# A residual stream kept centered over channels in a two-layer hybrid block (state-space scan, attention, experts)

## The chip, the cores and the metric

The kernel runs on one core of one Trainium2 chip. The metric is the device time of one launch in microseconds. Five engines work side by side, each on its own instruction list, in order: TensorE (PE, matmuls; PEld are its weight loads), VectorE (DVE), ScalarE (ACT), GpSimd (POOL) and SyncE (SP). SP issues plain transfers; POOL issues those that add to what is already at their destination ("adds" below) and those that gather rows by index. All arithmetic is in float32.

## The reference

The input is x of shape (8, 256, 32, 32): 8 images, 256 channels, 1024 tokens each. Layer 0 is a selective-scan block and a feed-forward block, layer 1 is attention and a mixture of experts. Cut to what matters here:

```
x1 = x  + mamba(layernorm(x)) @ W_out        # layernorm "a"; scan over tokens, 512 x 16 states
x2 = x1 + gelu(layernorm(x1) @ W1 + b1) @ W2 + b2          # layernorm "f"
t  = x2 + attention(layernorm(x2)) @ Wo + bo               # layernorms "t" (here) and "x" (below)
n  = layernorm(t)
out = t + layernorm(n + sum of 2 experts of n) * gamma + beta   # layernorm "y"
```

Every layernorm runs over the 256 channels of one token: it subtracts the mean, squares, takes the mean of the squares, and multiplies by one over its root. The two experts are chosen once for each image, from the mean of n over its tokens.

## The kernel before

**Tiling.** Channels lie on the 128 partitions, two blocks of them (KC = 2). Tokens are cut in 16 chunks of 512 (CH; two for each image, chunk i = 2b + c), so an activation is a [128, 2, 512] tile of 512 KB. Such tiles come from one pool, `t4`, of 25 slots; a stream of work that needs slots declares how many it will hold at most (`Owner`). The scan keeps its products in 4 slots of another pool (`hb`).

**The recurrence sets the order.** The main loop (lines 2018 to 2051) walks over 16 chunks x 32 steps; a step is one of 16 states for half of the 512 inner channels. In each step DVE multiplies the inputs by B (`hb<-xm,bc`), scans over the tokens (`hb<-da_all,hb`), and multiplies by C (`hb<-hb,bc`); POOL adds the result to the accumulator `dx` in SBUF by a transfer; ACT makes the decays `da_all` two steps ahead; SP loads the rows B and C, spread over the partitions, two states ahead (`bc<-bc_d`).

**All else is fitted around it by a planner.** The rest of the program consists of Python generators ("streams"): `prologue` (layernorm a, input product, convolution, softplus, once a chunk), `park` (layernorm a and the gate for chunks 2 to 15, early, results to DRAM), `epilogue` (gate product, W_out, layernorm f, feed-forward, layernorm t), `attention` and `project_part` / `project_last` (Wo, layernorm x), `all_experts` and `finish` / `finish_last` (layernorm y, output). While the program is written out, a small model (lines 62 to 124) keeps a clock for each queue; each `yield` says when the stream may go on, and `advance` (line 1908) issues what is due between two DVE instructions of the recurrence. Where the model finds PE idle, `keep_warm` (line 1894) issues a small matmul without use ("warm"). The model's times fix only the order; on the chip, semaphores decide. `all_experts` (line 1979) starts the experts of an image once the `o` streams (project) of both chunks have ended.

**Four tables** (lines 266 to 269), one entry a chunk, say at which step the next chunk's prologue starts (FRONT), at which the gate is fetched (GATE), whether the convolution runs on PE instead of DVE (CONV, `conv_pe` against `conv_dve`: 12 multiply-adds on DVE), and whether a softplus term is added by transfers alone (SOFT: 3 adds for each half instead of 2, and no DVE instruction).

**The layernorm** (line 390) works with the channels on the partitions, so the mean is a matmul with a constant matrix (`mean_w`, 1/256), spread over all partitions at once; DVE subtracts it; ACT squares; eight small matmuls put the variance of 512 tokens into a 128 x 128 block; ACT and DVE make 1/sqrt there; four matmuls with `pick` spread it over the partitions again; DVE multiplies. For f, t and x outside the last chunk the input is a sum made by an add into SBUF, and is stored to DRAM for the next residual (`stored`); the square overwrites it, and so waits for that store (lines 409 to 411). The last chunk (i = 15) and the last image keep their sums in SBUF and add on DVE.

The input x enters the residual twice: layernorm a reads it, and `epilogue` adds it by a transfer (line 952: `pool.dma_start(out=x1, in_=x_v[b, :, :, tok], accum_op=ALU.add)`).

Of the kernel before, what the change touches and what calls it, by code (L numbers as in the profile page):

```python
# [17 lines left out]
P = 128  # L18
# [36 lines left out]
def hybrid_kernel(ctx: ExitStack, tc: tile.TileContext, a: dict, out: bass.AP):  # L55
# [131 lines left out]
    for q in range(4):  # L187
        pool.memset(pick[HD * q : HD * q + 1, q : q + 1], -0.5)
    eps_t = const.tile([P, 1], F32, name="eps_t")
# [28 lines left out]
    b1 = const.tile([P, HID // P], F32, name="b1")  # L218
# [8 lines left out]
    bo2 = const.tile([P, KC], F32, name="bo2")  # L227
# [8 lines left out]
    t_d, xf_d, x1_d = {}, {}, {}  # L236
# [29 lines left out]
    FRONT = (7, 1, 1, 1, 1, 10, 16, 3, 14, 1, 10, 1, 13, 1, 13)  # L266
    GATE = (20, 7, 29, 25, 29, 21, 20, 15, 18, 30, 25, 28, 25, 14, 26, 15)
    CONV = (0, 0, 1, 1, 1, 1, 0, 0, 0, 0, 0, 0, 0, 0, 0, 0)
    SOFT = (0, 1, 1, 1, 1, 1, 0, 0, 0, 1, 0, 1, 1, 0, 1, 0)
# [120 lines left out]
    def layernorm(  # L390
        tmp, bank, src, dst, name, gain=None, bias=None, sums=None, stored=None, centered=False
# [4 lines left out]
        if stored is not None:  # L396
            dst = yield from tmp.take(f"{dst}_{name}")
        if not centered:
# [6 lines left out]
            if stored is None:  # L405
                yield
        if stored is None:
            sq = yield from tmp.take(f"sq_{name}")
        else:
            yield max(stored, model.end)  # L410
            sq = src
        act.activation(sq, dst, AF.Square)
# [26 lines left out]
        yield  # L439
        if gain is None and sums is None:  # L440
            vec.tensor_tensor(dst, dst, ps.unsqueeze(1).to_broadcast([P, KC, CH]), ALU.mult)
        else:
            for k in range(KC):
                vec.scalar_tensor_tensor(
                    dst[:, k, :], dst[:, k, :], 1.0 if gain is None else gain[:, k : k + 1], ps,
                    ALU.mult, ALU.mult, accum_out=None if sums is None else sums[:, k, :],
                )
                if bias is not None:
                    vec.tensor_scalar(
                        dst[:, k, :], dst[:, k, :], bias[:, k : k + 1], None, ALU.add  # L450
                    )
        bank.put(ps)
        tmp.put(sq)
        return dst
# [21 lines left out]
    set_up, gates_ready = [], []  # L476
# [84 lines left out]
    def prologue(i: int):  # L561
# [7 lines left out]
        if i < PARK:  # L569
            yield sp.dma_start(xn, x_v[b, :, :, c * CH : (c + 1) * CH])  # L570
            yield from layernorm(mem, banks, xn, xn, f"a{i}")
# [257 lines left out]
    def park():  # L829

        for i in range(PARK, B * NCH):
# [6 lines left out]
            yield from layernorm(mem, banks, xn, xn, f"a{i}")  # L838
# [61 lines left out]
    def epilogue(i: int):  # L900
# [7 lines left out]
        while "sz" not in me:  # L908
# [21 lines left out]
        if last:  # L930
            yield sp.dma_start(x1, x_v[b, :, :, tok])
# [14 lines left out]
        yield  # L946
        mem.put(*y)
        if last:
            xn = yield from mem.take(f"x_{i}")
            yield from layernorm(mem, banks, x1, xn, f"f{i}")  # L950
# [1368 lines left out]
```

## Time and profile before

| what | value |
| --- | --- |
| time, median of 3 runs | 3439.8 us (3434.69 to 3441.22) |
| profiled execution: its own time / its span | 3450.06 us / 3448.1 us |
| DVE, PE, ACT, POOL busy | 3031.7, 3192.0, 2459.8, 1127.5 us |
| PE busy in warm matmuls (`warm<-mean_c,zero_c`) | 352.6 us |
| first recurrence step, last one | 77 us, 3062 us |
| attention of image 0 to 7, first matmul at | 666, 1012, 1364, 1727, 2092, 2467, 2835, 3151 us |
| routing of the last image (logits) | 3347 us |
| bytes moved by transfers | 642.22 MB |

The profile is one execution. A group row names line, engine, operation, output tile<-input tiles, shapes, the count, then busy time and the mean of one instruction, then how long the engine stood idle just before them and who ended that. Nearly all rows have line 98 or 95, that of the helper through which the planner issues, so the tile names tell what it is: `mu_f`, `mu_t`, `mu_x`, `mu_a` are the means of the layernorms, `var_…` their variances. DMA shares are the mean busy share of 16 engines; packets overlap a little, so that a short stretch can show more than 1.

### The profile page before, as it was taken

To read this page: it belongs to the slowest core of one execution; us is meant where nothing else is said; L and a number is where in the kernel's file an instruction comes from. 1 tells how busy PE (TensorE), PEld (TensorE's weight loads), DVE (VectorE), ACT (ScalarE), POOL (GpSimd) and SP (SyncE) were. 2 spreads that over 40 slices of the span, in tenths; PEclk is the share of its full clock that TensorE was granted. 3 is DMA by queue.
4 is the path that set the end of the run, shared out by engine and by line. 5 is a ranking of instruction groups with operands and counts; after the bars stand their busy time and mean duration, and the time that the engine had idled before them with its cause. 6 is when DMAs were issued, how large, how long until landed. Compare 5 with 4: busy or idle time off the path is not lost. (4 is left out here: it accounts for less than half of the span.)

```text
span 3448.1 us, 40234 instructions
## 1 busy us (share of the span) xinstructions
PE 3192.0 (93%) x14371; PEld 1355.8 (39%) x14371; DVE 3031.7 (88%) x3171; ACT 2459.8 (71%) x3550; POOL 1127.5 (33%) x1068
## 2 busy tenths in 40 slices
PE   7888889899999999999999998999999999999997
PEld 4544343433343334333443334334433343334343
DVE  5889999999999899999999999999999999972561
ACT  4665857578777887887778876887778768764643
POOL 0243224322542244233452244325542243311010
PEclk9889999899999999999999999999999999999999
DMA  3878999989998999898998989799889989971120
GB/s 105 222 170 204 213 224 214 226 206 228 196 206 185 210 203 218 181 210 198 228 207 188 221 196 222 187 215 207 193 189 209 202 191 199 225 160 61 32 77 23
DMA packets 233187, 642.22 MB, mean 186 GB/s; under 512 B 29520, under 2 KB 106000, under 8 KB 232976
## 3 DMA queue, kind: packets, MB, share of 16 engines
q0 software_dynamic: 138176, 371.52, 57.7%
q1 hardware_dynamic: 94800, 268.03, 23.5%
q8 instruction: 115, 1.88, 0.2%
q14 instruction: 96, 0.79, 0.1%
HBM read 253.33 MB, written 77.07 MB: 96 GB/s over the span
## 5 line engine op out<-in xcount | busy, mean ns | idle before, releaser
L95 POOL DMA_DIRECT2D dx<-hb x512 | 540.5, 1059 | 1567.2 <-DVE hb L98 1127.5
L98 ACT ACTIVATE da_all<-dt,vecs 128x512 f32<-128x512 f32 (+1 forms) x1024 | 698.1, 716 | 291.5 <-DVE hb L98 285.5
L98 DVE TENSOR_TENSOR hb<-xm,bc 128x1024 f32<-128x1024 f32 x512 | 617.0, 1205 | 28.1 <-DMA dx<-hb 27.5
L98 DVE TENSOR_TENSOR_SCAN hb<-da_all,state,hb 128x512 f32<-128x512 f32 x512 | 631.2, 1270 | 10.4 <-ACT da_all L98 10.4
L98 DVE TENSOR_TENSOR hb<-hb,bc 128x1024 f32<-128x1024 f32 (+1 forms) x512 | 624.9, 1220 | 0.0
L98 DVE TENSOR_TENSOR_SCAN hb<-da_all,hb 128x1024 f32<-128x1024 f32 x256 | 585.1, 2285 | 8.5 <-ACT da_all L98 8.5
L98 ACT ACTIVATE pt<-sc 128x1024 f32<-128x1024 f32 x512 | 494.2, 1017 | 84.3 <-PE sc L98 72.2
L98 POOL COPY state<-hb 128x2 f32<-128x2 f32 x256 | 339.3, 1332 | 238.1 <-DVE hb L98 211.0
L98 PE MATMUL warm<-mean_c,zero_c 128*128 128x256 f32 x1084 | 352.6, 446 | 63.6 <-ACT dt L98 13.8
L98 PE MATMUL sc<-qk,qk 32*128 32x512 f32 x2048 | 343.6, 644 | 21.9 <-ACT pt L98 18.2
L98 PEld LDWEIGHTS warm<-mean_c,zero_c 128*128 128x128 f32 x1084 | 205.7, 211 | 214.1 <-PE warm L98 80.5
L98 PE MATMUL num<-pt,v 128*32 128x512 f32 x2048 | 278.4, 614 | 11.9 <-DVE ot L98 11.8
L98 PE MATMUL fh<-x_f,w 128*128 128x512 f32 x480 | 232.4, 614 | 5.9 <-DVE x_f L98 3.2
L98 PE MATMUL den<-pt,ecb 128*32 128x512 f32 x1792 | 237.6, 601 | 0.0
L98 PE MATMUL facc<-fh,w 128*128 128x512 f32 x512 | 231.1, 598 | 5.4 <-ACT xp L98 1.7
L98 PE MATMUL re<-he,g 128*128 128x512 f32 x472 | 219.0, 609 | 6.5 <-ACT pt L98 2.3
L98 PE MATMUL he<-xe,g 128*128 128x512 f32 x448 | 217.6, 610 | 2.5 <-ACT he L98 2.2
L98 ACT ACT_TABLE_LOAD x159 | 204.0, 1283 | 3.5 <-PEq L2306 0.7
L98 PEld LDWEIGHTS sc<-qk,qk 32*128 32x128 f32 x2048 | 102.1, 183 | 211.9 <-ACT pt L98 93.0
L98 PEld LDWEIGHTS facc<-fh,w 128*128 128x128 f32 x512 | 95.0, 190 | 131.5 <-issue 118.8
L98 PEld LDWEIGHTS fh<-x_f,w 128*128 128x128 f32 x480 | 86.7, 192 | 138.3 <-issue 109.8
L98 PEld LDWEIGHTS re<-he,g 128*128 128x128 f32 x472 | 89.6, 195 | 126.5 <-issue 107.9
(376 smaller groups left out, 4326.7 us busy)
## 6 DMA issues: line engine op xcount, KB each, us to landing
bc<-bc_d SPq DMA_DIRECT2D x256, 512.0 KB, 4.9
dx<-hb POOLq DMA_DIRECT2D x256, 512.0 KB
dx<-hb POOLq DMA_DIRECT2D x256, 511.0 KB
dt<-e POOLq DMA_DIRECT2D x48, 512.0 KB
dt<-u POOLq DMA_DIRECT2D x30, 512.0 KB
sz_d<-sz SPq DMA_DIRECT2D x28, 512.0 KB, 4.4
sz<-sz_d SPq DMA_DIRECT2D x28, 512.0 KB, 11.4
xe<-xf_d SPq DMA_DIRECT2D x28, 512.0 KB
```

What stands on the lines that cost most here:

```text
L95: f(*args, **kw)
L98: return f(*args, **kw)
```

## The change

The residual is carried without its mean over the channels. Layernorm a subtracts the mean as before, but the centered x is also stored (`xc_d`) and is what `epilogue` adds. W_out, W2, Wo and the biases b2 and bo have their mean over the output channels taken out once, during setup, so all that is added to the residual is centered too; f, t and x then need neither the mean nor the subtraction, and their square goes to the destination tile instead of over the input, with no wait for the input's store. The mean of the true residual is a row of 512 numbers a chunk: layernorm a's mean, and the products of W_out's, W2's and Wo's column means (`wm_out`, `wm_2`, `wm_o`) with the same inputs, made by the new `means` on PE and ACT and put to DRAM (`mu_d`, three rows a chunk). `project` loads the first three, adds the last, and stores the total (`mus_d`). `finish` adds it, spread over the partitions, to the output as a further add; `project_last` adds it to t. The gain gamma of layernorm y goes from DVE's last step to ACT's scale beside beta in `finish`. `epilogue` may not begin before the weights are centered. The four tables have new entries. Some small constants share storage (`b1`, `bo2`).

```diff
-    FRONT = (7, 1, 1, 1, 1, 10, 16, 3, 14, 1, 10, 1, 13, 1, 13)
-    GATE = (20, 7, 29, 25, 29, 21, 20, 15, 18, 30, 25, 28, 25, 14, 26, 15)
-    CONV = (0, 0, 1, 1, 1, 1, 0, 0, 0, 0, 0, 0, 0, 0, 0, 0)
-    SOFT = (0, 1, 1, 1, 1, 1, 0, 0, 0, 1, 0, 1, 1, 0, 1, 0)
+    FRONT = (7, 1, 1, 4, 1, 12, 13, 1, 6, 1, 6, 1, 1, 1, 12)
+    GATE = (19, 7, 30, 22, 26, 19, 15, 19, 12, 30, 14, 30, 18, 22, 14, 13)
+    CONV = (0, 0, 1, 1, 1, 0, 0, 0, 0, 0, 0, 0, 0, 0, 0, 0)
+    SOFT = (0, 1, 1, 0, 1, 1, 0, 0, 0, 0, 0, 1, 0, 0, 1, 0)
...
-        if not centered:
+        if kept is not None:
+            mu = yield from bank.take(f"mu_{name}")
+            for k in range(KC):
+                for q in range(4):
+                    pe.matmul(
+                        mu[HD * q : HD * q + HD, :P], mean_w[:, :HD], src[:, k, q * P : q * P + P],
+                        start=(k == 0), stop=(k == KC - 1),
+                    )
+            yield
+            sq = yield from tmp.take(f"sq_{name}")
+            row = sq[:, 1, :P]
...
+            act.copy(row, mu[:, :P])
+            yield
+            for q in range(4):
+                pe.matmul(
+                    mu[:, q * P : q * P + P], pick[:, q : q + 1].to_broadcast([P, P]), row,
+                    start=True, stop=True,
+                )
+            landed = sp.dma_start(mu_row(kept, 0), row[::HD, :])
+            yield
+            vec.scalar_tensor_tensor(
+                dst, mu.unsqueeze(1).to_broadcast([P, KC, CH]), 2.0, src, ALU.mult, ALU.add
+            )
+            bank.put(mu)
+            yield model.end if kept < PARK else max(landed, model.end)
+            kept_at = sp.dma_start(xc_d[kept], dst)
+            src = dst
+        elif not centered:
...
-        if stored is None:
+            yield
+            src = dst
+        if kept is not None:
+            pass
+        elif src is dst:
             sq = yield from tmp.take(f"sq_{name}")
         else:
-            yield max(stored, model.end)
-            sq = src
-        act.activation(sq, dst, AF.Square)
+            sq = dst
+        act.activation(sq, src, AF.Square)
...
+    def means(bank, wm, tiles, name, row, bias=None, more=()):
+        ps = yield from bank.take(f"mean_{name}")
+        n = KC * len(tiles)
+        for d in range(n):
+            for q in range(4):
+                pe.matmul(
+                    ps[HD * q : HD * q + HD, :P], wm[:, d : d + 1].to_broadcast([P, HD]),
+                    tiles[d // 2][:, d % 2, q * P : q * P + P],
+                    start=(d == 0), stop=(d == n - 1 and not more),
+                )
+        for w, r in more:
...
+        yield
+        if bias is None:
+            act.copy(row, ps[:, :P])
...
+        bank.put(ps)
+        yield
...
-        while "sz" not in me:
+        while "sz" not in me or not centered_w:
             yield POLL
...
-            yield pool.dma_start(out=x1, in_=x_v[b, :, :, tok], accum_op=ALU.add)
+            yield
+            landed = pool.dma_start(out=x1, in_=xc_d[i], accum_op=ALU.add)
+            yield from means(banks, wm_out, y, f"m{i}", row)
+            mem.put(y[1])
+            mem.put(y[0], at=sp.dma_start(mu_row(i, 1), row[::HD, :]))
+            yield max(landed, model.end)
...
+        for w, wm, n in ((w_out, wm_out, ND), (w2, wm_2, HID // P), (wo, wm_o, KC)):
+            for k in range(n):
+                act.activation(
+                    w[:, k, :], w[:, k, :], AF.Identity, accum_out=wm[:, k : k + 1]
+                )
+            act.activation(wm, wm, AF.Identity, scale=1.0 / C)
+            act.activation(wm_neg[:, :n], wm, AF.Identity, scale=-1.0)
+            for k in range(n):
+                act.activation(
+                    w[:, k, :], w[:, k, :], AF.Identity, bias=wm_neg[:, k : k + 1]
+                )
+            yield
+        centered_w.append(True)
...
     def project(tmp, bank, b: int, c: int, x1, ot, n):
         xr = yield from tmp.take(f"xr_{n}")
+        yield sp.dma_start(xr[:12, 0, :P], mu_d[b * NCH + c].rearrange("n (q t) -> (n q) t", t=P))
+        row = xr[:, 1, :P]
+        yield from means(
+            bank, wm_o, [ot], f"o{n}", row, mean_b, [(pick3[:12, :], xr[:12, 0, :P])]
+        )
+        yield sp.dma_start(mus_d[b][c].rearrange("(q t) -> q t", t=P), row[::HD, :])
...
         sp.dma_start(xf_d[b][c], xf)
+        parts = yield from mem.take(f"parts_{n}")
+        yield sp.dma_start(
+            parts[:12, 0, :P], mu_d[b * NCH + c].rearrange("n (q t) -> (n q) t", t=P)
+        )
+        row = parts[:, 1, :P]
+        yield from means(
+            banks, wm_o, [ot], f"o{n}", row, mean_b, [(pick3[:12, :], parts[:12, 0, :P])]
+        )
...
+        landed = sp.dma_start(mu_s.rearrange("(q t) -> q t", t=P), row[::HD, :])
+        mem.put(parts, at=landed)
+        yield landed
+        pool.dma_start(
+            out=t, in_=mu_s.partition_broadcast(P).unsqueeze(1).to_broadcast([P, KC, CH]),
+            accum_op=ALU.add,
+        )
...
-        yield from layernorm(mem, banks, r, r, f"y{b}_{c}", V("gamma"), centered=True)
+        yield from layernorm(mem, banks, r, r, f"y{b}_{c}", centered=True)
         yield
         for m in range(KC):
-            act.activation(r[:, m, :], r[:, m, :], AF.Identity, bias=V("beta", m))
+            act.activation(
+                r[:, m, :], r[:, m, :], AF.Identity, bias=V("beta", m), scale=V("gamma", m)
+            )
         yield
         yield pool.dma_start(out=r, in_=t_d[b][c], accum_op=ALU.add)
+        mu_s = mus_d[b][c].partition_broadcast(P)
+        yield pool.dma_start(
+            out=r, in_=mu_s.unsqueeze(1).to_broadcast([P, KC, CH]), accum_op=ALU.add
+        )
```

The excerpt of `means` leaves out the two adds of further rows by `pick3`; W2's part of `epilogue` is changed in the same way as W_out's.

## The prediction

> **What bounds the kernel now.** I read the page's busy shares and slices first. VectorE (DVE) is at 88% of the span, and nearly full from the third slice to the 35th; the DMA engines are nearly full over the same slices; both drop in the last five.
>
> ```profile
> DVE  5889999999999899999999999999999999972561
> DMA  3878999989998999898998989799889989971120
> ```
>
> Busy time by stretch (us, PE, PEld, DVE, ACT, POOL, clock, DMA share, GB/s) turns this into three stages:
>
> ```profile
> 77.00:850.00 773.00, 679.95 (x3054) 328.76 (x3053) 725.58 (x721) 532.54 (x839) 243.25 (x246) 0.93 0.89 210
> 850.00:2000.00 1150.00, 1102.95 (x5146) 433.23 (x5144) 1105.87 (x1087) 902.39 (x1283) 447.49 (x404) 0.98 0.91 204
> 2000.00:3063.00 1063.00, 998.53 (x4350) 402.51 (x4350) 1008.18 (x1002) 809.07 (x1143) 403.06 (x369) 0.97 0.90 203
> 3063.00:3448.00 385.00, 356.21 (x1604) 157.07 (x1596) 155.58 (x299) 184.65 (x240) 32.00 (x34) 0.98 0.21 55
> ```
>
> From 77 to 3063 us DVE works 2839.6 of 2986 us (95%). PE looks as busy, but 352.6 us of the whole are its warm matmuls, which are filler. So the main stage runs at DVE's pace, with the DMA engines close behind; the last 385 us are a chain over PE with DVE mostly idle. The groups by shape price what the change touches on DVE (count | busy, mean ns | idle before):
>
> ```profile
> L98 DVE SCALAR_TENSOR_TENSOR xm<-xp,vecs,xm 128x512 f32<-128x512 f32 x144 | 97.7, 745 | 11.9 <-ACT xm L98 11.9
> L98 DVE SCALAR_TENSOR_TENSOR re<-re,vecs,var_y 128x512 f32<-128x512 f32 x28 | 19.5, 740 | 7.8 <-PE var_y L98 7.7
> L98 DVE TENSOR_TENSOR x_f<-x,mu_f 128x1024 f32<-128x1024 f32 x15 | 18.1, 1207 | 2.2 <-PE mu_f L98 2.2
> L98 DVE TENSOR_TENSOR tn_t<-fo,mu_t 128x1024 f32<-128x1024 f32 x15 | 18.1, 1206 | 1.6 <-PE mu_t L98 1.6
> L98 DVE SCALAR_TENSOR_TENSOR e<-u,e 128x1024 f32<-128x1024 f32 x14 | 17.1, 1222 | 6.8 <-ACT u L98 6.8
> L98 DVE TENSOR_TENSOR xf_x<-xr,mu_x 128x1024 f32<-128x1024 f32 x14 | 17.0, 1213 | 8.8 <-PE mu_x L98 7.7 <-issue 1.2
> ```
>
> The waits say that DVE is paced by itself: others wait for it, and it seldom for a transfer (the last line).
>
> ```profile
> ACT da_all L98 <- DVE hb L98: 285.5, 234, 9.1
> POOL dx L95 <- DMA dx<-hb: 236.7, 59, 8.2
> DVE hb L98 <- DMA dx<-hb: 27.5, 18, 3.4
> ```
>
> In the chain that ended last, the last token chunk's third layernorm and the routing after it stand in the open (start, us, what):
>
> ```profile
> 3336.85 2.00 PE mu_x L98 x4
> 3338.87 1.23 DVE xf L98
> 3340.12 1.06 ACT sq_x L98
> ...
> 3347.01 0.34 PE logits L98 x4
> ```
>
> **What the Trainium skill says.** "DMA: Bandwidth & Descriptors", section "Issuing engines are not separate DMA queues": transfers from SP and POOL run on the same 16 engines. The trace agrees: q0 (POOL) and q1 (SP) take 57.7% and 23.5% of one set of 16, so a new SP store competes with POOL's adds. "VectorE: DVE Perf Modes", section "The perf-mode tier table": fp32 tensor_tensor runs in the 1x mode, with a PSUM operand too. The trace agrees: 1024 columns cost 1207 ns with PSUM and 1205 ns without. "Perfetto Trace Analysis", section "Optimization Strategy": the most-contended engine can change from one regime of a kernel to the next. The trace agrees: DVE is at 95% until 3063 us and at 40% (155.58 of 385) after it.
>
> **The change, part by part.**
>
> *Subtractions.* f, t and x lose theirs: 44 in the main stage, 18.1+18.1+17.0 = −53.2 us of DVE. Layernorm a keeps one, as a scalar_tensor_tensor (1222 against 1215 ns): +0.1. The gain in y's last step moves into ACT's scale: 28 x 740 ns (19.5 busy) become 14 full-width multiplies at 1.21 = 17.0: −2.5.
>
> *Tables.* CONV[5] goes from 1 to 0: 12 taps on DVE x 745 ns = +8.9. SOFT goes to 0 for chunks 3, 9 and 12: 6 x 1222 ns = +7.3. DVE in all: −53.2+0.1−2.5+8.9+7.3 = −39.4. Do freed DVE microseconds shorten the stage? Chunks (one chunk is 32 recurrence steps) with 163 to 169 us of DVE lasted 168 to 179, those with 182 to 186 lasted 185 to 201: about one for one. I count them in full. DVE also waited 12.6 us ahead of these subtractions; a quarter of it I count as gone, −3, since the next instruction inherits most.
>
> *DMA.* A q0 packet of 4096 bytes took 334 ns and one of 2048 took 194, so a 512 KB add is 128 x 334/16 = 2.67 us of all engines, or 256 x 194/16 = 3.10 if cut at 2 KB. SP stores: 128 x 195/16 = 1.56. Added: 16 stores of centered x (25.0) and 14 broadcast adds of the mean row (2 KB source rows, 43.4). Saved: 6 adds by SOFT (−16.0), and 15 residual adds reading the 4 KB-contiguous copy instead of the input (−6.5). Net +46 us. The stretches give 773 x 0.89 + 1150 x 0.91 + 1063 x 0.90 = 2691 of 2986, a share of 0.90; it becomes 2737/2947 = 0.93. They hide behind DVE while the engines have room. Ten-microsecond slices of the packet records reach 1.08 (packets overlap), so full is about there: 0.83 of full goes to 0.86. DVE's waits for transfers (27.5 for dx<-hb, 5.4 and 4.0 ahead of the gate product and of xm x dt: 37 us) grow with the queue, 0.86/0.14 over 0.83/0.17, by a quarter: +9. Bounds: 0 if all hides, +46 if the DMA engines set the pace.
>
> *PE and ACT.* Mean rows: 16+32+12 = 60 small matmuls a chunk. The nearest row is the variance's eight 128x32x128 at 9.5/15 = 0.63 us, so 4.7; removed means 3 x 2.0. At the slower 1.09 seen for eight it is 8.2. So −1.3 to +2.2 a chunk, behind DVE. ACT gains four row copies of 0.31 us a chunk; a's Square now waits for a mean-row store, with da_all's exponentials queued behind it on ACT and DVE's scans behind those. Against that, the Squares of f, t and x no longer wait for a 512 KB store (x1m_d 6.9 us to landing). Unknown sign; +3, bounds −8 to +15.
>
> *POOL and SP.* Mean adds: 14 x 1.42 us of POOL (the x<-in_x row, also 2 KB pieces), less 6 x 1.06 and 15 x 0.36: +8 us on an engine at 33%. Behind each stand dx adds; they free hb. Six SP issues a chunk (0.4 each) go ahead of some bc loads, which are issued two states (four recurrence steps) early. Hidden; uncovered, they would cost 2.4 us a chunk.
>
> *Setup.* Centering 14 weight columns: 14 x (446+190+500) ns = 16 us of ACT near 307 us, W2's 9 us in one piece with da_all behind; two steps of decay (10 us) cover most: +3. At the start the packed mean (1.1 us against 3.8 at the cold clock) pays for ACT's row copy and the spread back: −0.5.
>
> *The end.* Last chunk: without mean and subtraction f saves 3092.84−3088.9 = 3.9, t 1.98+1.22 = 3.2, x 3340.12−3337.15 = 3.0. Mean matmuls queue ahead of the next matmuls: +0.7 (f), +1.9 (t: 32 x 0.079 against 1.22 of cover). Experts of the last batch start when project_last is done, and that now ends after a load, mean matmuls, a row store and both landings: about 10 us of the planner's time, which it fills with warm matmuls at some 60% that PE must really run ahead of the logits. I take +7 (floor 4: a 2.8 us small landing as for bc_d, plus 1). Sum −0.5, say 0; bounds −8 to +12.
>
> **Sum** on the profiled span 3448.1 (execution 3450.06): −39.4−3+9+3+3−0.5+0 = −28, giving 3420. That execution lies 10.3 us above the median 3439.8, so the median becomes 3412.
>
> **Rivals.**
> 1. *The DMA engines become the bound* (slower). Place: 350 to 3063 us. In 45% of ten-microsecond slices their share is already over 0.97. If they pace the steps, DVE's 39 us buy nothing and +46 comes onto the path, less some overlap: 3439.8+30 = 3470. It decides if they can't sustain 0.93. Against it: over 1600 to 1700 us the mean was 1.005 while DVE kept going.
> 2. *The planner gives it back.* The order is made anew and streams hold t4 buffers longer (xr and r through extra transfers); half the gain goes: 3439.8−6 = 3434, near no change.
> 3. *More is gained.* Without store waits f and t shorten each epilogue by some 8 us, attention starts earlier, and less of it hangs over into the last stage: attention of batch 6 ended at 3088, after the last step: 3390.
> 4. *That the change doesn't do what it says*: the subtraction of a is still there, so a quarter of the means stays; already in the sum.
>
> **Chances.** Forecast (3397 to 3429) 0.60; rival 1 0.14; rival 2 0.12; rival 3 0.14. Changes under 0.2% (6.9 us) can't be told from none. Faster 0.60+0.14+0.04 of rival 2 = 0.78; same 0.06; slower 0.14+0.02 = 0.16. Range: 0.60 + 0.12 + half of rival 3 makes eight in ten: 3390 to 3447; the forecast's own is 3397 to 3429.
>
> **What would show it.** Right: no mu_f, mu_t, mu_x groups; DVE near 2990 us in all; the last recurrence step 25 to 40 us before 3063; DMA share near 0.93; DVE's waits for dx<-hb under 50 us; a last stage of 385, with 10 us between xf and logits. Wrong: DVE idle in the main stage 30 us above its 146, behind DMA (rival 1) or behind ACT and PE (rival 2).

## Result and profile after

The changed kernel takes 3461.26 us (median of 4 runs, 3459.36 to 3467.59) where the kernel before took 3440.07 beside it: ratio 1.0062, 95% interval 1.0047 to 1.0078. It is 21 us slower; the forecast was 28 us faster, and the range ended at 3447. The profiled execution has a span of 3465.8 us, against 3448.1.

The page's slices of the changed kernel (DVE busy, DMA engines busy, in tenths) look like those of before: both nearly full up to the 35th slice.

```profile
DVE  5888999999899999999999989999899999952551
DMA  3887999989898999789997999799989998862140
```

The same stretches as in the prediction, cut at this kernel's own first and last recurrence step (us, PE, PEld, DVE, ACT, POOL, clock, DMA share, GB/s):

```profile
72.00:850.00 778.00, 679.56 (x3616) 333.68 (x3615) 718.36 (x717) 534.91 (x887) 259.69 (x243) 0.90 0.88 209
850.00:2000.00 1150.00, 1067.97 (x5448) 437.24 (x5447) 1087.34 (x1070) 896.00 (x1294) 445.68 (x402) 0.97 0.91 207
2000.00:3065.00 1065.00, 993.88 (x5121) 407.48 (x5124) 998.74 (x993) 813.72 (x1171) 420.82 (x374) 0.96 0.91 207
3065.00:3466.00 401.00, 374.30 (x1828) 170.49 (x1820) 149.63 (x292) 197.02 (x257) 41.75 (x43) 0.98 0.27 65
```

DVE works 2804.4 us in the first three rows, 35 less than the 2839.6 before. Yet they last 2993 us where they lasted 2986: DVE's idle time went from 146 to 189. The last stage went from 385 to 401. The groups by shape show that DVE's work changed as reckoned (count | busy, mean ns | idle before):

```profile
L98 DVE TENSOR_TENSOR hb<-xm,bc 128x1024 f32<-128x1024 f32 x512 | 616.2, 1203 | 62.7 <-DMA dx<-hb 35.1 <-issue 27.4
L98 DVE SCALAR_TENSOR_TENSOR xm<-xp,vecs,xm 128x512 f32<-128x512 f32 x156 | 105.8, 743 | 10.3 <-ACT xm L98 10.3
L98 DVE SCALAR_TENSOR_TENSOR e<-u,e 128x1024 f32<-128x1024 f32 x20 | 24.9, 1243 | 5.4 <-ACT u L98 5.4
L98 DVE TENSOR_TENSOR re<-re,var_y 128x1024 f32<-128x1024 f32 x14 | 17.0, 1213 | 8.9 <-PE var_y L98 8.5
```

The groups of mu_f, mu_t and mu_x are gone. The first row is where idle time appears: DVE stood 62.7 us ahead of the product that opens a recurrence step, 28.1 us in the kernel before:

```profile
L98 DVE TENSOR_TENSOR hb<-xm,bc 128x1024 f32<-128x1024 f32 x512 | 617.0, 1205 | 28.1 <-DMA dx<-hb 27.5
```

The waits (engine, what it waited for: us, times, longest) say the same from the other side: POOL waits 334 us for its own additions into dx, 237 before.

```profile
POOL dx L95 <- DMA dx<-hb: 334.2, 86, 10.0
ACT da_all L98 <- DVE hb L98: 338.3, 229, 8.8
DVE hb L98 <- DMA dx<-hb: 35.1, 17, 5.7
DVE hb L98 <- issue: 27.4, 11, 5.2
```

In the chain that ended last (start, us, what), the routing of the last image has lost the mean product and the subtraction, and gained a wait for the row of means:

```profile
3351.19 1.06 ACT xf L98
...
3356.02 1.32 DVE xf L98 x4
3357.38 3.31 PE warm L98 x14
3360.69 0.92 PE mean_o L98 x24
3361.62 2.93 PE warm L98 x12
3364.55 0.36 PE logits L98 x4
```

From the start of the Square to the logits it is 13.4 us; before, from the start of the mean product to the logits, 10.2.

### The profile page after: what moved, and what is told of

Its sections match the earlier page's. It is cut to its first block, busy times and chain, and to the rows that moved or that the text cites. A ratio compares the mean times of both kernels' runs of the same rounds, so it can differ in the third digit from the quotient of the medians.

```text
span 3465.8 us, 44262 instructions
## 1 busy us (share of the span) xinstructions
PE 3166.2 (91%) x16259; PEld 1381.6 (40%) x16259; DVE 2990.6 (86%) x3134; ACT 2472.3 (71%) x3656; POOL 1169.6 (34%) x1078
## 4 chain that ended last, share of the span: by engine, by line
PE 34%; DVE 26%; DMA 14%; ACT 14%; issue 9%; POOL 2%; DVEq 0%; SPq 0%; POOLq 0%; ACTq 0%
DVE hb L98 20%; DMA dx<-hb 13%; PE warm L98 4%; PE sc L98 3%; PE num L98 3%; PE fh L98 3%; PE he L98 3%; ACT L98 3%; PE re L98 3%; ACT da_all L98 2%; PE facc L98 2%; DVE xm L98 2%; PE den L98 2%; ACT fh L98 2%; PE halves L98 1%
## 5 line engine op out<-in xcount | busy, mean ns | idle before, releaser
L98 DVE TENSOR_TENSOR hb<-xm,bc 128x1024 f32<-128x1024 f32 x512 | 616.2, 1203 | 62.7 <-DMA dx<-hb 35.1
L98 POOL COPY state<-hb 128x2 f32<-128x2 f32 x256 | 375.4, 1470 | 218.5 <-DVE hb L98 201.5
L98 PE MATMUL warm<-mean_c,zero_c 128*128 128x256 f32 x1020 | 339.7, 453 | 56.2 <-ACT dt L98 15.6
L98 PEld LDWEIGHTS warm<-mean_c,zero_c 128*128 128x128 f32 x1020 | 193.9, 213 | 201.2 <-PE warm L98 78.6
L98 PE MATMUL he<-xe,g 128*128 128x512 f32 x448 | 223.5, 624 | 10.2 <-ACT he L98 5.0
```

What stands on the lines that cost most here:

```text
L98: return f(*args, **kw)
```

## Experiments

Ratios are to the kernel before on the same chip, with 95% intervals; microseconds worked out from them use 3440 us. The stages named below are read from DVE's recurrence steps in each trace: chunk 0, chunks 1 to 15, and what follows the last step.

In most of the kernels the order of the instructions is held. `planned(f, ...)` lets the planner cost an instruction as ever but doesn't issue it (`plain` issues it as usual); an instruction issued through `nc.vector` or `nc.gpsimd` is one that the planner doesn't know of. So every other instruction stays where it was in its queue, and one part of the change is measured without a new plan.

The expectations name the theories by letters: T, the added transfers lost the time; O, the order and the tables; S, chunk 0 and the last stage; A, the pace of ACT and PE; P, the new products on PE; W, the change's own work on PE and ACT.

### The added transfers, in the changed kernel's order

```diff
-        yield pool.dma_start(
+        yield planned(
+            pool.dma_start,
             out=r, in_=mu_s.unsqueeze(1).to_broadcast([P, KC, CH]), accum_op=ALU.add
         )
```

> The changed kernel with the 14 additions of the mean row in finish costed in the plan but not issued, so every other instruction keeps its place in its queue; the outputs of images 0 to 6 lack their means. Theory T (the added transfers queue up and give the gain back): these adds are the dearest of the new transfers, 14 x about 2.9 us of all 16 DMA engines, bunched where the experts of an image finish; the time falls by 12 to 35 us, to about 3426 to 3449, and the waits for transfers in chunks 1 to 15, 77 us in the changed kernel, fall to 40 to 60. Theory O (the new order and tables lost the time): within 6 us of 3461. Theory S (the first chunk and the last stage lost it): within 8 us of 3461, since the last stage holds few of these adds.

Measured: 1.0016 (1.0004 to 1.0029), 16 us under the changed kernel's 1.0062, inside theory T's 12 to 35.

```diff
-            kept_at = sp.dma_start(xc_d[kept], dst)
+            kept_at = planned(sp.dma_start, xc_d[kept], dst)
...
-            landed = pool.dma_start(out=x1, in_=xc_d[i], accum_op=ALU.add)
+            landed = pool.dma_start(out=x1, in_=x_v[b, :, :, tok], accum_op=ALU.add)
```

> The changed kernel with the 16 stores of the centered x costed in the plan but not issued; the residual is added from x itself, so the layernorms f, t and x see an x that is not centered and the output is wrong by that. Theory T: 16 x about 2 us of all DMA engines, but most of it before 980 us, while the parked chunks are made; the time falls by 3 to 15 us, to 3446 to 3458. Theories O and S: within 5 us of 3461.

Measured: 1.0042 (1.0026 to 1.0058).

The third kernel does both, and each small load and store of a row of means is `planned` too, with the small products that read a loaded row.

> The changed kernel with none of the transfers that the change added: no additions of the mean row, no stores of the centered x (the residual is added from x), no mean rows stored or loaded. Their plan stays, PE's and ACT's work for the means too; the means are missing from the outputs. Theory T: back to the gain that the freed DVE time should give, less chunk 0 and the last stage: 3415 to 3440, waits for transfers in chunks 1 to 15 near the 36 us of the kernel before. Theories O and S: no lower than 3450.

Measured: 1.0012 (1.0003 to 1.0021). So the transfers cost 0.50%, 17 us, in this order, and nearly all of it is the 14 additions of the mean row (16 us); leaving out the stores alone gives 7 us back, with an interval that reaches nothing. Theory T had 21 to 46 us for all of them, theories O and S at most 11; neither holds. Without any of them the kernel is still no faster than before, with 41 us less work on DVE. The transfers are most of the 21 us by which the changed kernel is slower, but only a third of the 49 us by which it missed the forecast. Most of DVE's idle time ahead of the opening product stays without them, 49.4 of 62.7 us:

```profile
L106 DVE TENSOR_TENSOR hb<-xm,bc 128x1024 f32<-128x1024 f32 x512 | 615.9, 1203 | 49.4 <-DMA dx<-hb 25.2
```

### The subtractions and their mean products, in the order of before

```diff
+            skip = name[0] in "ftx"
             for k in range(KC):
-                pe.matmul(mu, mean_w, src[:, k, :], start=(k == 0), stop=(k == KC - 1))
+                (planned if skip else plain)(
+                    pe.matmul, mu, mean_w, src[:, k, :], start=(k == 0), stop=(k == KC - 1)
+                )
             yield
-            vec.tensor_tensor(dst, src, mu.unsqueeze(1).to_broadcast([P, KC, CH]), ALU.subtract)
+            (planned if skip else plain)(
+                vec.tensor_tensor, dst, src, mu.unsqueeze(1).to_broadcast([P, KC, CH]),
+                ALU.subtract,
+            )
```

> The kernel before with the mean products and the subtractions of the layernorms f, t and x costed in the plan but not issued (48 of each; the layernorms leave the mean out). No transfer is added and nothing moves: this is the freed DVE time alone. If DVE is the bound of the recurrence, as the prediction had it, 53 us less on DVE give 40 to 56 us: 3385 to 3400. If transfers, PE and ACT bound the stage as much, less than half of it: 3415 or more.

The mean products go with the subtractions (94 us in PE's groups), and the squares go to the destination tile, with no wait for the input's store. Measured: 0.9916 (0.9902 to 0.993), 29 us: just over half of the 54 us by which DVE's busy time fell (3031.7 to 2977.6). From 3440 us that is 3411, in neither theory's range and nearer to the second's. The stage from chunk 1 to the last step (columns as above), in the kernel before:

```profile
322.00:3062.00 2740.00, 2573.40 (x11398) 1041.77 (x11398) 2616.12 (x2529) 2085.19 (x2970) 1002.59 (x926) 0.97 0.92 206
```

and without the subtractions:

```profile
322.00:3040.00 2718.00, 2518.57 (x11214) 1016.09 (x11218) 2567.85 (x2486) 2078.15 (x2970) 967.43 (x926) 0.96 0.92 208
```

DVE has 48 us less to do, and the stage is 22 us shorter: its idle time went from 124 to 150 us. Is it the transfers that take the other half? Two kernels leave out the 42 additions in finish, one with and one without the subtractions:

```diff
-        yield pool.dma_start(out=r, in_=y, accum_op=ALU.add)
-        yield pool.dma_start(out=r, in_=xf_d[b][c], accum_op=ALU.add)
+        yield planned(pool.dma_start, out=r, in_=y, accum_op=ALU.add)
+        yield planned(pool.dma_start, out=r, in_=xf_d[b][c], accum_op=ALU.add)
...
-        yield pool.dma_start(out=r, in_=t_d[b][c], accum_op=ALU.add)
+        yield planned(pool.dma_start, out=r, in_=t_d[b][c], accum_op=ALU.add)
```

> The kernel before with the three additions in finish (of the other expert's part, of xf and of t_d; 42 in all, some 2.9 us of all DMA engines each, 122 us) costed in the plan but not issued; the outputs of images 0 to 6 lack these terms. A control for the next kernel: what these transfers cost while DVE does all its subtractions. Theory T (transfers wait only where they crowd): 5 to 20 us less than 3445. Theory A (the stage is paced by ACT and PE once DVE has less to do): 0 to 10 us less.

> The kernel before without the mean products and subtractions of f, t and x (as in the run before_no_subtraction, which gave 0.9916 of the time before), and without the 42 additions in finish. If transfers ate the other half of the 53 us of DVE time (theory T), the subtractions are worth more here than the 29 us they were worth with all the additions: 38 to 50 us against the kernel before with fewer adds. If ACT, PE or the order took it (theory A), they are worth 22 to 33 us here too.

Measured: 0.9945 (0.9925 to 0.9965) and 0.9845 (0.9827 to 0.9864). The additions alone are worth 19 us, in theory T's range. Without them the subtractions are worth 1.0%, 34 us with 9 either way, just above theory A's range; the interval reaches theory T's too, and the 29 us of before. Even with 127 us less for the DMA engines to do (packet times 2808.8 to 2681.4 us), some 20 us of the freed 54 are not gained.

### Chunk 0 and the last stage

Chunk 0 lasted 258 us in the changed kernel's trace and 245 before; the last stage was 15 us longer. Two kernels took one suspect each. In the first the mean of layernorm a goes to DVE by the old way:

```diff
-                    pe.matmul(
+                    planned(
+                        pe.matmul,
                         mu[HD * q : HD * q + HD, :P], mean_w[:, :HD], src[:, k, q * P : q * P + P],
                         start=(k == 0), stop=(k == KC - 1),
                     )
+                nc.tensor.matmul(mu, mean_w, src[:, k, :], start=(k == 0), stop=(k == KC - 1))
...
-            vec.scalar_tensor_tensor(
+            planned(
+                vec.scalar_tensor_tensor,
                 dst, mu.unsqueeze(1).to_broadcast([P, KC, CH]), 2.0, src, ALU.mult, ALU.add
             )
+            nc.vector.tensor_tensor(
+                dst, src, mu.unsqueeze(1).to_broadcast([P, KC, CH]), ALU.subtract
+            )
```

> The changed kernel with the mean of the layernorm a made as in the kernel before: two products with the column of 1/C straight into the bank that DVE subtracts from, in place of eight products, a copy on ACT and four products; the plan is held, the copy of the row stays but off the path of DVE, and the rows stored are wrong. Theory S (chunk 0 lost 13 us because DVE now waits for a product, a copy and a second product ahead of each parked x): chunk 0 back to 244 to 250 us from 258, the time 6 to 14 us less than the changed kernel's, ratio 0.2 to 0.4 per cent lower. Theories T and O: within 4 us of the changed kernel.

Measured: 1.0043 (1.0027 to 1.0059), chunk 0 251 us. The gap to 1.0062, 7 us, is at the lower end of theory S's 6 to 14, but within the two intervals, and chunk 0 took 250 to 254 us in the first three kernels too, which have the longer route. So the route is not shown to cost anything. The 258 us stand beside a granted TensorE clock of 0.83 in that stretch; the only other trace with so long a chunk 0 (259 us, the next kernel) has 0.83 too, and the 18 others have 0.86 to 0.92 and 242 to 254 us. A part of the 13 us may be the clock of that one execution.

In the second the row of means of image 6 is made after its layernorm x:

```diff
-        yield sp.dma_start(xr[:12, 0, :P], mu_d[b * NCH + c].rearrange("n (q t) -> (n q) t", t=P))
-        row = xr[:, 1, :P]
...
-        yield sp.dma_start(mus_d[b][c].rearrange("(q t) -> q t", t=P), row[::HD, :])
+        if not late:
+            yield from mean_row(xr)
...
         tmp.put(xf, at=sp.dma_start(xf_d[b][c], xf))
+        if late:
+            parts = yield from tmp.take(f"parts_{n}")
+            yield from mean_row(parts)
+            tmp.put(ot, parts)
```

> The changed kernel with one thing moved, and for image 6 alone: the row of means of the projection (load of the parts, products, copy, store) after the layernorm x and not ahead of the products with Wo. Everything up to the projection of chunk 14 keeps its order. Theory S (this row and its two transfers hold back the logits of image 6 by 29 us, and its experts then run inside the last attention): the logits of image 6 come at about 50 us after the last step in place of 77, the last attention ends about 10 us earlier, the last stage is 381 to 388 us in place of 395, the time 6 to 13 us less than the changed kernel's. Otherwise: within 4 us.

Measured: 1.005 (1.0034 to 1.0066); the last stage didn't get shorter (400 us by its trace, 395 in the changed kernel's). The products with Wo came 17 us earlier, but the logits of image 6 came 75 us after the end of the last step, hardly sooner than the changed kernel's 77 (the kernel before has 48): the new plan put other streams in between. Theory S fell in this part.

### The plan

What had not been taken apart was the order itself. Four kernels are planned afresh. The first has the changed kernel's code and the four tables of before:

```diff
-    FRONT = (7, 1, 1, 4, 1, 12, 13, 1, 6, 1, 6, 1, 1, 1, 12)
+    FRONT = (7, 1, 1, 1, 1, 10, 16, 3, 14, 1, 10, 1, 13, 1, 13)
...
```

> The changed kernel with the four tables FRONT, GATE, CONV and SOFT of the kernel before; all else as in the change. Theory O (the new tables lost the time): ratio 0.994 to 1.001. Theories T, S and P (the added transfers, chunk 0 and the products for the rows lost it): the tables of before were not made for this program, ratio 1.003 to 1.015.

Measured: 1.02 (1.0178 to 1.0222), beyond the ranges of all theories. With the tables of before the changed program is 47 us slower than with its own, so it isn't the new tables taken alone that lost the time. The second is the kernel before with the subtractions really taken out of the code, so that the plan knows of it:

```diff
-        if not centered:
+        skip = name[0] in "ftx"
+        if not centered and not skip:
             mu = yield from bank.take(f"mu_{name}")
```

> The kernel before without the mean products and subtractions of f, t and x, as in the run before_no_subtraction (0.9916), but with the plan made for it, so that the other queues are ordered for the shorter DVE work; the means are missing from its layernorms. If it was the held order that gave only 29 of the 53 us (theory O): 0.984 to 0.989. If ACT, PE and the transfers pace the stage as much as DVE does (theory A): 0.989 to 0.995.

Measured: 1.0062 (1.0043 to 1.0081). The same work in the held order took 0.9916. The new plan alone made 1.5%, 50 us; neither theory had that. The stage from chunk 1 to the last step grew from 2718 to 2792 us, and DVE's idle time in it from 150 to 213:

```profile
317.00:3109.00 2792.00, 2567.49 (x11572) 1050.88 (x11572) 2578.38 (x2498) 2094.67 (x2990) 984.00 (x929) 0.96 0.90 204
```

The third and fourth are a version that carries the means on PE and needs no large transfer: the mean of x is taken off in the bank of W_out's product, and the rows of means come back in the bank of an uncentered Wo's product.

```diff
+    def add_row(ps, picks, rows):
+        for q in range(4):
+            pe.matmul(
+                ps[:, q * P : q * P + P], picks[:, q : q + 1].to_broadcast([picks.shape[0], P]),
+                rows, start=False, stop=(q == 3),
+            )
...
                     ps, w_out[:, d, m * P : (m + 1) * P], y[d // 2][:, d % 2, :],
-                    start=(d == 0), stop=(d == ND - 1),
+                    start=(d == 0), stop=False,
                 )
+            add_row(ps, pick1[:4, :], rows)
```

> A version with the means carried by PE and not by transfers, with the tables of the kernel before. The residual stays x (no store of a centered x): each product with the centered W_out adds a bank row of minus the mean of x (four products over a 4-row tile, from the stored row), so that f and t need no mean and no subtraction; the product with an uncentered Wo adds the three stored rows of means (four products over a 12-row tile), so that t_d holds the whole sum, finish adds nothing more, and x keeps its mean and subtraction. 32 of the 48 subtractions are gone and the transfers added are rows of 2 KB. If a freed subtraction is worth the 0.6 us that the run before_no_subtraction gave (29 us for 48), 32 give 19 us, less 4 to 10 us for the mean rows on PE and ACT: ratio 0.993 to 0.998. If the mean products and the longer stages on PE (theory P) cost as much as they free: 0.999 to 1.004.

> The same version with the four tables of the changed kernel. By theory O (the tables move the time by 10 us or more) it differs from the run with the tables of before by more than 0.3 per cent; else by less.

Measured: 1.0327 (1.0305 to 1.0349) and 1.0371 (1.0345 to 1.0397). Both are slower than either kernel, the first far beyond both its ranges, with DVE idle 242 and 230 us in chunks 1 to 15; they differ by 0.4%, as theory O had it. Since these runs change work and plan at once, they don't tell what carrying means on PE is worth.

Then the bare question: how much does the time hang on the order, when the work is the same? One entry of FRONT, by one step:

```diff
-    FRONT = (7, 1, 1, 1, 1, 10, 16, 3, 14, 1, 10, 1, 13, 1, 13)
+    FRONT = (7, 1, 1, 1, 1, 11, 16, 3, 14, 1, 10, 1, 13, 1, 13)
```

> The kernel before with one entry of FRONT moved by one step: the prologue of chunk 6 starts at step 11 of chunk 5 and not at step 10. The work is the same. By theory O the plans that follow differ and with them the time, by 0.3 per cent or more, more likely slower since the tables of before were set for its own plan; by theory W within 0.2 per cent.

> The changed kernel with its entry of FRONT for chunk 5 moved by one step, 12 to 13. By theory O it differs from the changed kernel's 1.0062 by 0.3 per cent or more, either way; by theory W within 0.2 per cent.

(In the second, 12 became 13 in the changed kernel's table.) Measured: 1.0247 (1.0233 to 1.0262) and 1.0193 (1.0176 to 1.021). Both are as theory O had it. One step on one entry costs the kernel before 85 us, four times what the change did; DVE has the same 3171 instructions, PE 164 more warm matmuls (1248 for 1084). The stage of the first:

```profile
317.00:3124.00 2807.00, 2605.27 (x11532) 1067.94 (x11536) 2620.02 (x2535) 2085.36 (x2975) 1016.61 (x927) 0.97 0.89 202
```

DVE's 2620 us are those of before (2616); its idle time is 187 us and not 124. The new idle time has no single source. Of DVE's waits (0.6, 4.0 and 2.7 us in the kernel before):

```profile
DVE hb L98 <- issue: 15.5, 5, 5.6
DVE xm L98 <- DMA dt<-u: 15.3, 2, 9.7
DVE x L98 <- PE mo L98: 12.3, 2, 12.1
```

A few stream steps stand where what they need comes late, and DVE stands with them. The lengths of the chunks are those of before up to chunk 4; from chunk 5, whose entry it was, nine of eleven are longer, the worst (chunk 13) 216 us in place of 182.

### The order apart from the work

One kernel has the order of the changed kernel and nearly the work of before; the next has the same without the subtractions.

```diff
-            act.copy(row, ps[:, :P])
+            planned(act.copy, row, ps[:, :P])
...
             sq = dst
+            nc.vector.tensor_tensor(
+                dst, src, zero_c.unsqueeze(2).to_broadcast([P, KC, CH]), ALU.subtract
+            )
-        act.activation(sq, src, AF.Square)
+        act.activation(sq, dst if sq is dst else src, AF.Square)
```

> The changed program's order and tables with nearly the work of the kernel before: of what the change added, the additions of the mean row, the stores of the centered x, all rows of means (products, copies, stores and loads) and the centering of the weights are costed in the plan but not issued, and the mean route of a is that of before; of what it took away, the 48 subtractions of f, t and x are issued again, uncosted, each a DVE instruction of the same size ahead of the square (their mean products are not). What is left of the change is the order. Theory O (the order lost it): 3465 to 3490, ratio 1.004 to 1.011. Theory W (the change's own work on PE and ACT lost it, the order is neutral): ratio 0.997 to 1.003.

> The same without the 48 DVE instructions. The subtractions should be worth 20 to 35 us here too. Against no_added_transfers (1.0012) it leaves out the rows' products and copies, the centering and the longer route of a: by theory O that is worth under 8 us, ratio 0.998 to 1.002; by theory W 20 us or more, ratio 0.990 to 0.995.

Measured: 1.0182 (1.0167 to 1.0197) and 1.0022 (1.0012 to 1.0032). The first, all three stages:

```profile
73.00:324.00 251.00, 207.14 (x1120) 116.60 (x1119) 222.76 (x280) 150.36 (x285) 87.47 (x89) 0.89 0.75 183
324.00:3094.00 2770.00, 2516.99 (x11008) 1013.84 (x11012) 2629.94 (x2544) 2071.60 (x2960) 1052.08 (x920) 0.95 0.89 203
3094.00:3505.00 411.00, 376.76 (x1660) 169.53 (x1652) 155.73 (x297) 195.87 (x252) 34.41 (x37) 0.96 0.21 55
```

and the second, the last two:

```profile
321.00:3053.00 2732.00, 2485.42 (x11014) 1004.40 (x11015) 2582.01 (x2501) 2069.75 (x2960) 1055.89 (x920) 0.96 0.90 205
3053.00:3447.00 394.00, 365.89 (x1660) 164.10 (x1652) 149.66 (x292) 195.65 (x252) 34.40 (x37) 0.99 0.22 58
```

In this order 48 DVE instructions are worth 1.6%, 55 us, all of their 54 us and not half. (Here the plan doesn't know of them and no mean products go with them, so the case is not quite that of the order of before.) And the rows of means, their products and copies, the centering of the weights and the longer route of a cost nothing that can be measured: with them 1.0012 (no_added_transfers), without them 1.0022. Theory W fell; theory O's ranges, 1.004 to 1.011 for the first kernel and 20 to 35 us for the subtractions, were too small.

### The change's content in the order of before

The last two complete the picture: the large transfers added to the kernel before, uncosted, with and without the subtractions.

```diff
         yield pool.dma_start(out=r, in_=t_d[b][c], accum_op=ALU.add)
+        mean = xf_d[b][c][0, 0, :].partition_broadcast(P)
+        nc.gpsimd.dma_start(
+            out=r, in_=mean.unsqueeze(1).to_broadcast([P, KC, CH]), accum_op=ALU.add
+        )
...
             stored = sp.dma_start(xn_d, xn)
+            nc.sync.dma_start(xc_d, xn)
```

> The order of the kernel before, without the mean products and subtractions of f, t and x (as in before_no_subtraction, 0.9916), and with transfers of the same size, number and place as the change's large ones, not costed in the plan: in finish one more addition of a broadcast row of 2 KB (14; a row of xf stands in for the row of means) and one more store of 512 KB beside each store of the normalized x (16). The layernorms leave their means out. If the transfers cost what they cost in the changed kernel, 0.5 per cent: ratio 0.994 to 0.999, so that the change in this order is a gain. If they cost more where the order leaves no place for them: 1.000 or more.

> The kernel before with the same 30 transfers added and nothing taken away. At 2.9 us of all DMA engines for an addition and 2 for a store they take some 75 us of the engines' 2799 busy. If they cost what the changed kernel showed: ratio 1.003 to 1.007. If DVE, with all its subtractions to do, hides them better than in the changed kernel: under 1.003. If they fall badly in this order: over 1.008.

Measured: 0.9914 (0.9896 to 0.9931) and 1.0042 (1.0026 to 1.0058). The stage of the first:

```profile
317.00:3046.00 2729.00, 2520.18 (x11214) 1017.25 (x11218) 2569.46 (x2486) 2077.90 (x2970) 974.30 (x937) 0.96 0.93 210
3046.00:3426.00 380.00, 353.08 (x1600) 155.90 (x1592) 150.64 (x295) 186.20 (x241) 35.84 (x38) 0.98 0.25 64
```

The first lies below its expected ranges: the DMA share is the forecast 0.93, and the transfers cost nothing there that can be measured (0.9914 against 0.9916). With the subtractions still to do, the same transfers cost 14 us, as expected. All together:

| order | subtractions | large transfers added | ratio |
| --- | --- | --- | --- |
| of before | yes | no | 1 |
| of before | yes | yes | 1.0042 |
| of before | no | no | 0.9916 |
| of before | no | yes | 0.9914 |
| of the changed kernel | yes | no | 1.0182 |
| of the changed kernel | no | no | 1.0022 |
| of the changed kernel, with the work for the rows | no | no | 1.0012 |
| the changed kernel | no | yes | 1.0062 |

The granted TensorE clock (the share of its full speed, averaged over a run) is a rival for part of these differences. In the 230 runs on record, each compared only with those of the same kernel in the same session, a mean clock lower by 0.001 goes with about 1.5 us more (correlation −0.61); what causes what is not shown. The kernels' means differ:

| pair | time | mean clock |
| --- | --- | --- |
| subtractions out, order of before | −29 us | 0.963 to 0.952 |
| the same, fewer additions | −34 us | 0.966 to 0.957 |
| subtractions out, changed order | −55 us | 0.941 to 0.950 |
| changed order for that of before, no subtractions | +36 us | 0.952 to 0.950 |
| new plan, kernel before without subtractions | +50 us | 0.952 to 0.956 |
| the whole change | +21 us | 0.963 to 0.954 |

An estimate with that slope makes the three values of the subtractions, at an equal clock, about 45, 47 and 42 us. So that their worth depends on the order is not shown; the clock alone could make the difference. The cost of a new order stays: the 36 us become about 33, the 50 us grow, and 8 of the 85 us of the moved entry would go (0.963 to 0.958). Of the whole change's 21 us, 13 could be the clock; what gives a kernel its mean clock was not tested.

No complete version measured here beats the kernel before. One that makes the whole change in the order of before, with the row work placed into it by hand, was not tried.

## Why the prediction was wrong

From before to after by the table, in microseconds: the subtractions out, order held, −29; the changed kernel's order and tables, +36 (1.0022 − 0.9916); the work for the rows, the centering and the route of a, −3; the added transfers in that order, +17. The sum is the measured +21, as it must be, since each step starts where the one before it ended; in another sequence the parts could differ. The step that failed is the **Sum**: it adds the parts with no term for the new order. That stood only as rival 2, "half the gain goes", with a chance of 0.12 and at 3434, which gives back 22 us (half of the 28 would be 14). In its place the runs show +36 us for the order and its tables. What the rival named is what happened, larger than it had it: it took back the whole gain, and the transfers then made a loss of it.

- **DVE's sum**: right as a sum, −41.1 busy (3031.7 to 2990.6) for −39.4. "I count them in full" was wrong: in the order of before 54 us of DVE time are worth 29, or some 45 at an equal clock by the estimate above. The argument for it, that chunks with more DVE work last longer by as much, compares chunks that were planned with that work in them; it doesn't say what the other engines do when work is taken out between them.
- **The tables**: the +16.2 us of DVE work were counted, and the traces have them: the groups of xm and e grew by 8.1 and 7.8 us. That the tables and the new plan order everything else too was not.
- **Transfers**, +9 with bounds 0 and +46: 0, 14 and 17 us in three settings, so the bounds held and the value was low for this order. The packet time of q0 and q1 rose by 38 us (2798.9 to 2837.0) for the reckoned 46. "DVE's waits for dx<-hb under 50" came true to the letter, at 35.1, while 27.4 us more stood under another name, "issue". Of these 62.5 us the changed order has 49.2 without any added transfer (25.2 and 24.0), so the transfers account for some 13 and the order for the rest of the growth from 28.1. POOL's longer wait for its own additions is no measure of lost time: it is 300.5 us in the order of before with the transfers, at 0.9914. Rival 1, that the DMA engines set the pace, is wrong: at a share of 0.93 the kernel ran at 0.9914.
- **PE, ACT, setup, start**, +5.5 together: measured −3, with an interval of about 5 us each way; inside the bounds, below the value. The two kernels' mean clocks differ (0.950 and 0.956); at an equal clock the estimate is +6.
- **The end**, 0: wrong by 15 us of span, though its own terms were good. For the last routing it had −3 and +7; the chain shows +3.2, and 7.2 us between xf and the logits. The rest goes with the order: the last attention begins 3 us later after the last step and takes some 8 us longer, with more of the experts of image 6 inside it (64 of their products `he` from its start to the last routing, 48 in the kernel before). The last stage is 394 us without any added transfer or row work in this order, and 380 in the order of before with all the large transfers (both by the stretches above).
- **Rival 3** (3390): no sign of it; attention began 3 us later after the last step, not earlier.
- **The signs**: the last recurrence step was to come 25 to 40 us earlier and came at 3065 instead of 3063. DVE's idle time, 43 us above 146, passed the mark of "wrong". The reckoning has two slips that don't matter: 32 x 0.079 less 1.22 is 1.3 and not 1.9, and the ten-microsecond slices from 350 to 3063 us reach 1.10, with 49% of them over 0.97, where it has 1.08 and 45%.

The forecast, 28 us for the whole change, is almost what the change's content gives in the held order (0.9914, 30 us). That is partly luck: that kernel has no new tables, no rows and no centered weights, and the subtractions were taken at nearly twice what they were worth in it.

Open is why the order of the changed kernel is the worse one, place by place. Part of the 36 us is DVE work: 13 us more (2990.2 against 2977.6), from CONV and SOFT less the gain moved to ACT. Part stands in the last stage (11 us by the traces of the two kernels without subtractions, 387.7 against 376.5 from the end of the last step); the waits of the rest are many and short. That each kernel's tables fit its own plan unusually well, those of before better, is argued from four changes of plan with the work the same or nearly so, which all cost time, 1.3 to 2.5%; it is not shown.

## What to carry to other kernels

Where a planner makes the order, a change to the code is two changes, the work and a new order, and the second can be the larger. Measure how much the time hangs on the order first (move one entry by one step), and measure the work apart from it, by leaving out instructions that the planner has costed, or issuing some that it doesn't know of. Set the mean granted clock of the runs beside such differences before reading them as the worth of an instruction. A gain of 1% by a sum over instruction times needs a term, and a range, for the order as soon as one entry's step moves the time by 2%.

## What the runs showed that was not expected

- One prologue begun one recurrence step later (an entry of 15) costs 1.3 and 2.5%, with the same instructions on DVE.
- 48 DVE instructions of 54 us are worth 29 us in one order and 55 in another, with mean granted clocks that move opposite ways and could make the difference. The 30 large transfers cost nothing, 14 or (with the small ones) 17 us.
- Within a kernel, a run with a mean clock lower by 0.001 takes about 1.5 us longer.
- In two executions the granted TensorE clock was 0.83 over chunk 0, which lasted 258 and 259 us; in 18 with 0.86 to 0.92 it lasted 242 to 254.
